# One second-layer tile of the last group but one, moved within the last group's V products

## The chip, the cores and the metric

The kernel runs on one core of one Trainium2 chip. The metric is the device time of one execution in microseconds (us). A core has five engines that run on their own and wait for each other through counters: TensorE (PE; its weight loads are shown as PEld), VectorE (DVE), ScalarE (ACT), GpSimd (POOL) and SyncE (SP), which here only issues copies. Each engine works through its own queue in order.

## The reference

The input x has 16 x 512 rows of 512 numbers. Each row carries a pathway number (0 to 499), a compartment number (0 to 4) and a mask bit; each batch entry has three condition vectors.

```
h = ln(x, pw_g[pathway], pw_b[pathway]);  h = ln(h, cp_g[compartment], cp_b[compartment])
t = ln(x, tm_g[compartment], tm_b[compartment])
m, n, r = x + mlp_ln(condition)            # one vector per batch entry and condition
s = ln(x, ms_g[mask], ms_b[mask])
cat = concat(w0*h, w1*t, w2*m, w3*n, w4*r, w5*s)        # w = softmax(aw)
out = x + ln(silu(cat @ W1 + b1) @ W2 + b2) * g + be    # W1: 3072 x 512, W2: 512 x 512
```

All is in float32. The kernel does not form the concatenation. What depends on x alone goes through one 512 x 512 matrix (the X product: the weighted sum of three blocks of W1); t and s are the same normalized x times table rows, so for rows of one (compartment, mask) pair they go through one blended matrix (the V product); h goes through its own block (the H product). What is left, constant for a pair and a batch entry, is one row that is added.

## The kernel before

The 8192 rows are sorted by (mask, compartment) pair and cut into 16 groups of 512 rows (`sts`, one state per group); a group is worked on as four tiles of 128 rows (`NJ` = `Q` = 4). A preparation, ordered by a list of pieces written out by hand, sorts the rows, computes tables and conditions, and does the first two groups. A loop of 16 steps per group does the next ones (`step`), and `last_window` does the last group, number 15, together with what is left of group 14. The schedule is manual: instructions stand in each engine's queue in the order in which the program emits them, and the framework adds the waits.

The first layer of a group is twelve products, X, V and H for each of its four tiles: `layer1` (L300, matmul in L305), four matrix instructions of a 128 x 128 block against 128 x 512 each, which show as eight records in the profile. They accumulate in one PSUM tile per row tile; the result is complete after the H product. The left operands (`cX`, `cV`, `cH`) are transposed rows; VectorE transposes 32 x 32 blocks into `rX`, `rV`, `rH`, and SP copies them into place, 16 copies of 64 KB per operand (`spread`, L164).

The V product of tile g needs the blended matrix for that tile, in four parts: ScalarE writes one scaled table block (`s_part`, L190), VectorE multiplies and adds the other (`build`, L196). Two buffers `vs` serve for this; in the last group the third matrix lies in a buffer of x that is free by then (it appears as `xbs`).

The hidden tile takes its gathered row (`hidden_add`, L309), SiLU (L312), a transposition and a spread into `cZ`; the second layer (`layer2`, L322, matmul in L324) makes four matrix instructions per tile, against W2, into another PSUM pool of four buffers. After it come an addition (L327), the sum of squares on ScalarE (L332), the inverse root on GpSimd (L345, a power), scale and residual on VectorE, and an indirect output from GpSimd (`put_out`, L358). GpSimd also adds the output offset to x in place, once per tile (`shift_x`, L294), and issues the gathers (L130).

In `last_window` the steps s = 0 to 11 emit the products X0 to X3, V0 to V3, H0 to H3 of group 15. `end_hidden` at step 0 finishes group 14's hidden tiles and spreads its `cZ`. The builds for V1 and V2 are emitted in step 3, that for V3 in step 6; the shifts of the four tiles in steps 4 to 7, each after the gather of steps 3 to 6. The nested function `finish` does everything from the second layer to the output for one tile. For tile 0 of group 14 it is called at step 8, before H0 is emitted; for the other three, and for the four of group 15, behind the loop.

Of the kernel before, what the change touches and what calls it, by code (L numbers as in the profile page):

```python
# [52 lines left out]
def kernel(ctx: ExitStack, tc: tile.TileContext, a: dict, out: bass.AP):  # L53
# [26 lines left out]
    NJ = S // P  # L80
# [78 lines left out]
    def spread_row(st, rot, cat, blk, g):  # L159

        if cat not in st:
            st[cat] = catp.tile([P, Q, NC, P], F32, tag=f"cat{blk}", name=f"{cat}{st['w']}")
        for q in range(Q):
            nc.sync.dma_start(st[cat][q * L : (q + 1) * L, g].rearrange("p c t -> p (c t)"),  # L164
                              st[rot][g * L : (g + 1) * L, q].rearrange("p c j t -> p (c j t)"))

    def spread(st, blk):
        for g in range(Q):
            spread_row(st, "r" + blk, "c" + blk, blk, g)
# [15 lines left out]
    def s_part(st, g, at=None):  # L185

        w = st["w"]
        st["v", g] = v = vs[(Q * w + g) % 2] if at is None else at
        for c in range(NC):
            nc.scalar.activation(v[:, c], ws[:, c], AF.Identity, scale=scs[:, c, g, w : w + 1])  # L190

    def build(st, g):
        w = st["w"]
        v = st["v", g]
        for c in range(NC):
            nc.vector.scalar_tensor_tensor(v[:, c], wt[:, c], sct[:, c, g, w : w + 1], v[:, c], ALU.mult, ALU.add)  # L196

    def gather_add(st, g):
        w = st["w"]
        st["add", g] = t = gp.tile([P, D], F32, tag="add", name=f"add{w}_{g}", bufs=4)  # L200
        gather(t, rows_2[:, :], i_add[:, g, w : w + 1])
# [76 lines left out]
    def front_a(st, j):  # L278
        norm_n(st, j)
        front_1(st, j)  # L280
        front_pow(st, j)

    def front_b1(st, j):
        front_mean(st, j)
        front_norm(st, j)

    def front_b2(st, j):
        pw, cp = st.pop(("g", j))
        nc.vector.tensor_mul(pw[:, :D], pw[:, :D], cp)  # L289
        turn_to(st, "rH", "H", j, pw[:, :D])  # L290

    def shift_x(st, j):

        nc.gpsimd.tensor_add(st["xb"][:, j, :], st["xb"][:, j, :], rows[:, 2, :])  # L294


    def psum(k, name):
        return (ps_1, ps_2)[k].tile([P, D], F32, tag=("p1", "p2")[k], name=name)

    def layer1(st, blk, g):  # L300
        if blk == "X":
            st["p1", g] = psum(0 if st["w"] == 0 else 1, f"p1_{st['w']}_{g}")
        m = {"X": wx_, "V": st.get(("v", g)), "H": wh_}[blk]
        for c in range(NC):
            nc.tensor.matmul(st["p1", g], st["c" + blk][:, g, c, :], m[:, c, :],  # L305
                             start=(blk == "X" and c == 0), stop=(blk == "H" and c == NC - 1))
# [7 lines left out]
    def hidden(st, g):  # L314
        hidden_add(st, g)
        hidden_silu(st, g)

    def turn_z(st, g, blk="Z"):
        turn_to(st, "rZ", blk, g, st["add", g])

    def layer2(st, j):
        st["p2", j] = p2 = psum(0, f"p2_{st['w']}_{j}")  # L322
        for c in range(NC):
            nc.tensor.matmul(p2, st["cZ"][:, j, c, :], w2[:, c, :], start=(c == 0), stop=(c == NC - 1))  # L324
# [9 lines left out]
    def last_a(st, j):  # L334
        last_add(st, j)
        last_sum(st, j)
# [10 lines left out]
    def last_std(st, lo=0, hi=NJ):  # L347
        last_var(st, lo, hi)
        last_pow(st, lo, hi)
# [6 lines left out]
    def put_out(st, j):  # L356
        w = st["w"]
        nc.gpsimd.indirect_dma_start(out_rows, bass.IndirectOffsetOnAxis(ap=tok[:, j, w : w + 1], axis=0),  # L358
                                     yb[:, j, :], None)
# [52 lines left out]
    for nm in ("mem", "noi", "res"):  # L412
        k = a[nm + "T"].shape[0]
# [479 lines left out]
    def end_hidden(st, older):  # L893

        last_b(older, 3)
        hidden(st, 3)
        turn_z(st, 2)
        turn_z(st, 3)
        spread(st, "Z")
# [86 lines left out]
    def last_window(older, prev, st):  # L986

        def finish(done, j):

            y = yb[:, j, :]  # L990
            layer2(done, j)
            last_a(done, j)
            yg = gp.tile([P, D], F32, tag="cp", name=f"yg{done['w']}_{j}")
            nc.vector.tensor_mul(yg, y, rows[:, 1, :])
            last_std(done, j, j + 1)
            nc.vector.scalar_tensor_tensor(y, yg, done["rsy"][:, j : j + 1], done["xb"][:, j, :], ALU.mult, ALU.add)
            put_out(done, j)

        for s in range(13):
            if s == 8:  # L1000
                finish(prev, 0)
            if s < 12:
                layer1(st, "XVH"[s // 4], s % 4)
            if s == 0:
                end_hidden(prev, older)
            elif s == 1:
                put_out(older, 2)
                front_a(st, 2)
                s_part(st, 2, older["xb"])
            elif s == 2:  # L1010
                put_out(older, 3)
                front_b1(st, 2)
                front_a(st, 3)
                front_b2(st, 2)
            elif s == 3:
                front_b1(st, 3)
                build(st, 1)
                front_b2(st, 3)
                spread(st, "H")
                build(st, 2)  # L1020
            elif s == 5:
                s_part(st, 3, vs[Q * st["w"] % 2])
            elif s == 6:
                build(st, 3)
            elif s >= 9:
                hidden(st, s - 9)
                if s >= 10:
                    turn_z(st, s - 10, "V")
            if 3 <= s < 7:
                gather_add(st, s - 3)  # L1030
            if 4 <= s < 8:
                shift_x(st, s - 4)
        turn_z(st, 3, "V")
        for g in range(Q):
            spread_row(st, "rZ", "cZ", "V", g)
        for j in range(1, NJ):
            finish(prev, j)
        for j in range(NJ):
            finish(st, j)

    for w in range(2, NW - 1):
        for s in range(16):
            step(s, *sts[w - 2 : w + 3])
    last_window(*sts[NW - 3 : NW])


# [51 lines left out]
```

## Time and profile before

| | us |
|---|---|
| median of 3 runs | 1045.17 (1044.87 to 1051.08) |
| profiled execution | 1045.43 |
| its span, first to last instruction | 1043.4 |
| TensorE busy in the span | 994.1 (95%) |
| VectorE, ScalarE, GpSimd busy | 877.9, 572.7, 572.2 |
| mean granted TensorE clock | 0.982 of full |
| last group's X products begin | 960.05 |
| last product ends | about 1033 |

A row of the order-of-time view has the start in us from the span's start, the length in us, the engine, the line, the operation, "written tile <- read tiles" with the size, and the number of instructions merged; in brackets stands the engine's idle time just before and what ended it. Ends of matrix instructions are modelled, so starts are the firmer numbers. SP's copies are shown as SPq. Busy time on GpSimd is rough.

### The profile page before, as it was taken

The page shows a single profiled execution, that of the slowest core. Times are in us where ns is not written, and L with a number is a line of the kernel's source. Part 1 is how long each engine was busy: PE and PEld are TensorE (multiplying, and loading weights), DVE is VectorE, ACT ScalarE, POOL GpSimd, SP SyncE. Part 2 cuts the span into 40 slices and gives each one's busy share as a digit, 9 for nine tenths or more (in the row PEclk, how much of TensorE's full clock was granted, in tenths as well). Part 3 has the DMA queues.
Part 4 walks back from the last instruction along what each step waited for, and adds up shares of the span by engine and source line. Part 5 has one row for each costly group of instructions (what it writes and reads, how often), then busy time and mean ns, then how long its engine had stood idle before and what let it go on. Part 6 is the DMA issues. An engine that isn't in the chain of part 4 may idle for free.

```text
span 1043.4 us, 11015 instructions
## 1 busy us (share of the span) xinstructions
PE 994.1 (95%) x2523; PEld 450.3 (43%) x2523; DVE 877.9 (84%) x1577; ACT 572.7 (55%) x1153; POOL 572.2 (55%) x573
## 2 busy tenths in 40 slices
PE   5989699899999999999999999999999999999896
PEld 5634244343344444444444444444444444444342
DVE  7978889888889888888888888888888989888844
ACT  2698684483746473646464555546374647364311
POOL 3764652645656574737464646555565656473413
PEclk9979999899999999999999999999999999999998
DMA  9595887666767585767666676667677768585512
GB/s 276 196 269 159 236 260 218 166 182 184 197 182 215 160 232 157 226 166 205 174 199 181 193 188 192 183 203 190 194 195 193 200 171 227 154 229 152 146 35 91
DMA packets 95655, 197.66 MB, mean 189 GB/s; under 512 B 26290, under 2 KB 26290, under 8 KB 95592
## 3 DMA queue, kind: packets, MB, share of 16 engines
q0 software_dynamic: 32096, 108.55, 36.4%
q1 hardware_dynamic: 62230, 87.44, 30.3%
q10 hardware_dynamic: 1266, 0.99, 0.3%
q8 instruction: 21, 0.34, 0.1%
q14 instruction: 42, 0.34, 0.1%
HBM read 104.14 MB, written 21.44 MB: 120 GB/s over the span
## 4 chain that ended last, share of the span: by engine, by line
PE 70%; DVE 11%; DMA 4%; ACT 4%; issue 4%; SPq 3%; POOL 2%; POOLq 0%; DVEq 0%; ACTq 0%
PE p L305 48%; PE p L324 16%; SPq L164 3%; PE pe L811 3%; DVE vs L196 3%; PE pn L574 2%; DVE pw L289 1%; DMA xbs<-in_mem_W 1%; ACT vs L190 1%; ACT pw L276 1%; DVE add L309 1%; DVE yb L353 1%; DMA add<-rows,i_add 1%; POOL xbs L130 1%; DVE pw L260 1%
## 5 line engine op out<-in xcount | busy, mean ns | idle before, releaser
L305 PE MATMUL p<-vs,cV 128*128 128x512 f32 x504 | 229.6, 600 | 5.6 <-DVE vs L196 5.6
L324 PE MATMUL p<-w,cZ 128*128 128x512 f32 x512 | 228.9, 592 | 0.0
L305 PE MATMUL p<-wx__82,cX 128*128 128x512 f32 x512 | 225.8, 599 | 2.0 <-DVE add L309 2.0
L305 PE MATMUL p<-wh__83,cH 128*128 128x512 f32 x512 | 222.8, 592 | 0.0
L196 DVE SCALAR_TENSOR_TENSOR vs<-wt,sct,vs 128x512 f32<-128x512 f32 x252 | 206.3, 877 | 0.0
L190 ACT ACTIVATE vs<-ws,scs 128x512 f32<-128x512 f32 x252 | 160.7, 707 | 2.6 <-PE pe L811 2.1
L269 POOL TENSOR_TENSOR rsh<-veh,mhalf 128x1 f32<-128x1 f32 x64 | 46.0, 719 | 198.0 <-DVE veh L265 190.1
L305 PEld LDWEIGHTS p<-wx__82,cX 128*128 128x128 f32 x512 | 98.2, 192 | 125.7 <-issue 119.0
L305 PEld LDWEIGHTS p<-vs,cV 128*128 128x128 f32 x504 | 95.7, 192 | 130.5 <-issue 95.1
L324 PEld LDWEIGHTS p<-w,cZ 128*128 128x128 f32 x512 | 97.3, 190 | 122.6 <-issue 121.3
L305 PEld LDWEIGHTS p<-wh__83,cH 128*128 128x128 f32 x512 | 97.3, 190 | 122.5 <-issue 121.7
L276 ACT ACTIVATE pw<-pw,nmh,rsh 128x512 f32<-128x512 f32 x64 | 51.8, 809 | 128.4 <-DVE nmh L147 128.4
L312 ACT ACTIVATE add<-add 128x512 f32<-128x512 f32 x64 | 40.3, 630 | 145.4 <-DVE add L309 141.1
L358 POOL DMA_INDIRECT out<-yb,tok x64 | 68.5, 1070 | 64.4 <-DVE yb L353 27.5
L332 ACT ACTIVATE junk<-yb 128x512 f32<-128x512 f32 x64 | 40.1, 627 | 95.1 <-DVE yb L327 94.9
L130 POOL DMA_INDIRECT add<-rows,i_add x64 | 75.9, 1185 | 24.1 <-issue 9.1
L260 DVE TENSOR_TENSOR pw<-xn,pw 128x512 f32<-128x512 f32 x64 | 44.0, 688 | 48.5 <-ACT xn L237 48.5
L294 POOL TENSOR_TENSOR xbs<-xbs,rows 128x512 f32<-128x512 f32 x64 | 81.4, 1275 | 0.9
L130 POOL DMA_INDIRECT xbs<-in_x,tok x64 | 65.1, 1017 | 24.6 <-issue 18.0
L130 POOL DMA_INDIRECT cp<-cp_rows,i_cp x64 | 67.8, 1060 | 19.5 <-issue 19.2
L130 POOL DMA_INDIRECT pw<-in_pw,i_pw x64 | 64.0, 1000 | 20.9 <-issue 12.7
L237 ACT ACTIVATE xm<-xbs,mnm,mrs 128x512 f32<-128x512 f32 x64 | 48.6, 804 | 41.3 <-DVE rV L156 39.0
(234 smaller groups left out, 1236.8 us busy)
## 6 DMA issues: line engine op xcount, KB each, us to landing
cX<-rX SPq DMA_DIRECT2D x256, 64.0 KB
cV<-rV SPq DMA_DIRECT2D x256, 64.0 KB
cH<-rH SPq DMA_DIRECT2D x256, 64.0 KB
cZ<-rZ SPq DMA_DIRECT2D x256, 64.0 KB
cVe<-rVe SPq DMA_DIRECT2D x64, 64.0 KB
rows<-adde SPq DMA_DIRECT2D x14, 256.0 KB
w1x<-in_int_W SPq DMA_DIRECT2D x2, 1024.0 KB
ws<-in_int_W SPq DMA_DIRECT2D x1, 1024.0 KB
```

The costliest lines, as they stand in the source:

```text
L130: nc.gpsimd.indirect_dma_start(dst, None, table, bass.IndirectOffsetOnAxis(ap=idx, axis=0), **kw)
L190: nc.scalar.activation(v[:, c], ws[:, c], AF.Identity, scale=scs[:, c, g, w : w + 1])
L196: nc.vector.scalar_tensor_tensor(v[:, c], wt[:, c], sct[:, c, g, w : w + 1], v[:, c], ALU.mult, ALU.add)
L237: nc.scalar.activation(t, st["xb"][:, j, :], AF.Identity, bias=st[nm][:, j : j + 1], scale=st[rs][:, j : j + 1])
L260: nc.vector.tensor_mul(pw[:, :D], st.pop(("xn", j)), pw[:, :D])
L269: nc.gpsimd.tensor_tensor(rs, st.pop(("ve", j)), mhalf[:, :1], ALU.pow)
L276: nc.scalar.activation(pw[:, :D], pw[:, :D], AF.Identity, bias=st.pop(("nm", j)), scale=st.pop(("rs", j)))
L294: nc.gpsimd.tensor_add(st["xb"][:, j, :], st["xb"][:, j, :], rows[:, 2, :])
L305: nc.tensor.matmul(st["p1", g], st["c" + blk][:, g, c, :], m[:, c, :], start=(blk == "X" and c == 0), stop=(blk == "H" and c == NC - 1))
L312: nc.scalar.activation(st["add", g], st["add", g], AF.Silu)
L324: nc.tensor.matmul(p2, st["cZ"][:, j, c, :], w2[:, c, :], start=(c == 0), stop=(c == NC - 1))
L358: nc.gpsimd.indirect_dma_start(out_rows, bass.IndirectOffsetOnAxis(ap=tok[:, j, w : w + 1], axis=0), yb[:, j, :], None)
```

## The change

The call of `layer2` leaves `finish` and becomes a call of its own. For tile 0 of group 14 it is made at step 6, before V2 is emitted; the rest of `finish` for that tile is called at step 7, after V3 is emitted, where step 8 called all of it before H0. In the queues this gives:

- TensorE: the second-layer tile stands between V1 and V2; before, it stood between V3 and H0.
- VectorE and ScalarE: the same order as before.
- GpSimd: the power (L345) and the output (L358) of that tile stand ahead of the shift of group 15's fourth tile; before, they stood behind it.
- SP: the same order as before.

For the other seven tiles `layer2` is called directly before `finish`, in one loop in place of two, so their order is the same. The functions called are not altered.

```
         def finish(done, j):
             y = yb[:, j, :]
-            layer2(done, j)
             last_a(done, j)
...
         for s in range(13):
-            if s == 8:
-                finish(prev, 0)
+            if s == 6:
+                layer2(prev, 0)
             if s < 12:
                 layer1(st, "XVH"[s // 4], s % 4)
...
             elif s == 6:
                 build(st, 3)
+            elif s == 7:
+                finish(prev, 0)
             elif s >= 9:
...
-        for j in range(1, NJ):
-            finish(prev, j)
-        for j in range(NJ):
-            finish(st, j)
+        for k in range(1, 2 * NJ):
+            done, j = (prev, st)[k // NJ], k % NJ
+            layer2(done, j)
+            finish(done, j)
```

## The prediction

> **What bounds the kernel now.** The page first: which engine fills the span, and what the chain that ended last runs through.
>
> ```profile
> span 1043.4 us, 11015 instructions
> PE 994.1 (95%) x2523; PEld 450.3 (43%) x2523; DVE 877.9 (84%) x1577; ACT 572.7 (55%) x1153; POOL 572.2 (55%) x573
> ```
>
> TensorE is busy for 95% of the span, and the chain gives PE 70%. A change that keeps the number of products can win only where TensorE stands still, so the next view is the order of time on PE over the last group.
>
> ```profile
> 973.78 7.17 PE L305 MATMUL p<-vs,cV 128*128 128x512 f32 x16
> 982.52 1.98 PE L305 MATMUL p<-xbs,cV 128*128 128x512 f32 x4 [1.57 <-DVE xbs L196]
> 986.43 1.98 PE L305 MATMUL p<-xbs,cV 128*128 128x512 f32 x4 [1.93 <-DVE xbs L196]
> 988.25 3.60 PE L305 MATMUL p<-vs,cV 128*128 128x512 f32 x8
> 991.69 3.60 PE L324 MATMUL p<-w,cZ 128*128 128x512 f32 x8
> 995.12 13.90 PE L305 MATMUL p<-wh__83,cH 128*128 128x512 f32 x32
> 1008.85 24.20 PE L324 MATMUL p<-w,cZ 128*128 128x512 f32 x56
> ```
>
> The rows are V products 0 and 1, the first half of V2, its second half, V3, the second-layer tile in question, the four H products, and the seven remaining second-layer tiles. V2 waits twice for the build of its weights (L196 into xbs); everything else follows back to back. A tile takes 3.43 us (991.69 to 995.12; the H row gives 13.73 / 4). The idle times in brackets are counted against modelled ends, so I count starts: the last record of V1 starts at 980.36 and records follow each other every 0.43 us, so the next could start at 980.79. From there to the H products at 995.12 there are 14.33 us and three tiles of work (V2, V3, one second-layer tile), 10.30 us. TensorE loses 4.03 us here.
>
> Why does V2 wait? VectorE and GpSimd in the same stretch:
>
> ```profile
> 981.04 5.99 DVE L196 SCALAR_TENSOR_TENSOR xbs<-wt,sct,xbs 128x512 f32<-128x512 f32 x4
> 986.96 2.73 DVE L196 SCALAR_TENSOR_TENSOR vs<-wt,sct,vs 128x512 f32<-128x512 f32 x4
> 995.32 0.69 DVE L327 TENSOR_TENSOR yb<-p,rows 128x512 f32<-128x512 f32 x1 [5.63 <-PE p L324]
> ```
> ```profile
> 980.64 1.27 POOL L294 TENSOR_TENSOR xbs<-xbs,rows 128x512 f32<-128x512 f32 x1
> 982.07 1.25 POOL L130 DMA_INDIRECT add<-rows,i_add  x1 [0.16 <-issue]
> 983.33 2.49 POOL L294 TENSOR_TENSOR xbs<-xbs,rows 128x512 f32<-128x512 f32 x2
> 997.10 0.56 POOL L345 TENSOR_TENSOR rsy<-vey,mhalf 128x1 f32<-128x1 f32 x1 [11.28 <-DVE vey L340]
> ```
>
> The same four instructions take 2.73 us for V3's weights and 5.99 us for V2's. One by one: part 0 of V2 981.04 to 982.46 (1.42), part 1 982.39 to 983.13 (0.74), part 2 983.05 to 986.38 (3.33), part 3 986.30 to 987.04 (0.74). Both long ones end 0.55 to 0.56 us after a GpSimd addition of L294 does (981.91 and 985.82): VectorE waits for GpSimd's addition, and beside the indirect load (982.07) it does not. Part 2 waits out two additions, the third and the fourth shift of x, back to back.
>
> **The change, part by part.** *The second-layer tile goes ahead of V2.* The work on TensorE is the same, 3.43 us, at another place. Its weight load needs row 0 of cZ, whose four copies left SP from 966.77 on, 16 in 10.07 us, so by 969.3. SP issues without a gap although each copy waits for the eighth before it, so a copy lands within 8 x 0.63 = 5.0 us (an estimate from the rows of SP): 974.3, 6.5 us ahead of 980.79. Its PSUM buffer was last read by group 13's first second-layer addition, 937.00. So it runs from 980.79 to 984.22.
>
> *V2 behind it.* Part 0 of its weights is ready at 982.46, part 1 at 983.13: no wait at 984.22. Part 2 is wanted half a tile later, at 985.94. When is it ready? This depends on GpSimd, whose queue the change also alters.
>
> *finish moves from ahead of H0 to step 7.* Its VectorE instructions keep their place in that queue (behind the build of V3's weights, ahead of the first hidden addition), and ScalarE's too. On GpSimd the power of L345 and the output of L358 now stand ahead of the fourth shift. The power waits for VectorE, so the fourth shift no longer follows the third at 984.6. Part 2 is then blocked by one addition: 983.33 + 1.27 + 0.55 = 985.15. Part 3 follows at 985.8, V3's parts from 986.5 to 988.45.
>
> Here a rule bears on the sum. The Trainium skill (SBUF — State Buffer, Who interferes with whom) says that a VectorE instruction with two SBUF inputs and a GpSimd instruction that reads SBUF exclude each other, and that the one to issue first keeps the port for its whole length. The exclusion agrees with the rows; the order doesn't: part 2 is recorded at 983.05, the shift at 983.33, and it is part 2 that takes 3.33 instead of 0.74. By the rule part 2 would be ready at 983.8, by the row at 985.15. Both are before 985.94. If the block lasted as long as it does now (something other than the fourth shift), part 2 would be ready at 986.38, 0.4 late, plus about 0.2 for restarting (the first record after a wait is 0.1 longer): that is the upper bound, and V3 would start at 988.25 as now. I take the row.
>
> *The sum.* V2 984.22 to 987.65, V3 to 991.08 (its parts are wanted at 987.65, 988.5, 989.4, 990.2 and ready before), and H0 starts at 991.08 instead of 995.12: 4.04 us. With the block as now it starts at 991.69: 3.43 us.
>
> *What H wants.* Row 0 of cH leaves SP from 981.18, four copies by 983.7, landed by 988.7 by the same 5.0; the later rows need 2.5 us each and are consumed in 3.43. No wait.
>
> *finish's own chain.* From L327 to the end of its output it takes 995.32 to 999.77, 4.45 us, now beginning with the end of the V3 build, 988.45, to 992.9. VectorE is free at 991.6; the first hidden addition is wanted at 991.08 + 3.43 = 994.51, so 2.9 us of cover; without it each us late would move that addition, and VectorE stands idle for over 2 us before each of the next three. The fourth shift follows at 992.9 to 994.2 and is first wanted by the last tile's finish, over 30 us later. ACT, waiting for the same chain, has nothing queued that is wanted before H0 ends. Zero, and a gain isn't possible either, since no one on the path waits for these.
>
> *Rewritten loop.* The seven remaining tiles keep their order: zero.
>
> *What is late next.* From H0 on everything hangs on TensorE: four H products, hidden additions, the spread of cZ, seven tiles, and the outputs. The outputs start at 1015.92, 1019.97, 1024.02, 1027.65, 1031.23, 1034.85 and 1038.45, each only when the one before has landed (the second waits 1.70 for the transfer of the first), so the end is set by that series, not by the last product; but the series begins with tile 1 behind the H products, so it moves with them. I see nothing in it that is tied to an absolute time. The page's span 1043.4 becomes 1039.4; the profiled execution took 1045.43, 2.03 outside the span, and becomes 1041.4; it lies 0.26 above the median of the runs, 1045.17, which becomes 1045.17 - 4.04 = 1041.1.
>
> **The rivals.**
>
> *The block lasts as now*, 3.43 us of gain: 1041.7. For it: VectorE's record starts ahead of GpSimd's, so the account of which instruction holds what is not clean, and spans on GpSimd are rough. Against it: ends at 0.55 us after GpSimd's in both cases, and 0.61 in the build of V1's weights (977.66 to 979.82, addition to 979.21).
>
> *H0 becomes the wait.* Before, H0 is shown not to wait at 995.12, and nothing in the trace shows cH's landing. If it landed only around 993 to 995, between 2 us and nothing would remain: 1043 to 1045.2. Against it: SP's steady issue bounds the landing.
>
> *Slower.* TensorE runs in order, so a late operand of the moved tile holds V2, V3 and all H. The copies of cZ and cH count on the same completion counters; if the wait of the moved tile took in row 0 of cH as well, issued by 983.7, it would start at 986.6 with the 2.9 us that the outputs take to land, at 988.7 with 5.0; H0 10.30 us later, 996.9 to 999.0: 1.8 to 3.9 us slower, I take 1.8, 1047.0. It turns to slower when the tile starts later than 984.8. Against it: in earlier groups the same tile stands one product earlier (922.28, behind V0) and does not wait, with 16 copies of cZ issued from 911.82: 10.5 us after the first, here 14.
>
> *The change doesn't do what it says.* The built order shows it on TensorE, and the GpSimd swap, as described; only the gaps themselves could be a peculiarity of this execution, and then nothing is won: 1045.2. Since they follow from fixed orders of three queues, I put this with the second.
>
> **How the numbers follow.** Full gain 0.64 (1041.1); block as now 0.20 (1041.7); H0 waits or no gap 0.10 (1043 to 1045.2); slower 0.04 (1047.0); something else 0.02. The range reaches from 1040.3 (the full gain and the 0.12 that V1's last part waits, with 0.6 for the scatter of runs, of which the two lower ones lie 0.3 apart) to 1042.8 (the second case with the same scatter, and part of the third). All cases lie within 1%, 10.5 us, about what a measurement of this kernel can tell from no change: faster by more 0.01, within 0.97, slower by more 0.02.
>
> **What would show it.** In the changed kernel's profile: no idle time before the V2 products, the tile of L324 between V1 and V2, starting near 980.8; four xbs builds in about 4.8 instead of 5.99 us, none of 3.33; the fourth shift alone at about 993; H products near 991.1 without idle time; outputs 4 us earlier at equal distances. Wrong it would be if the moved tile waits, if xbs still shows a 3 us part, if idle time appears ahead of H0, or if the outputs' distances grow in exchange.

## The result, and the profile after

| | before | after |
|---|---|---|
| median of 20 runs each, us | 1045.24 (1042.10 to 1051.35) | 1039.88 (1035.46 to 1045.04) |
| ratio, 95% interval | | 0.9952 (0.9937 to 0.9967) |
| profiled execution, us | 1045.43 | 1036.91 |
| its span | 1043.4 | 1034.9 |
| TensorE busy in the span | 994.1 | 987.2 |
| mean granted TensorE clock | 0.982 | 0.988 |

The ratio puts the gain at 5.0 us, between 3.4 and 6.6. The prediction was a gain of 4.04 us, which lies in this interval; of its time, 1041.1 with a range from 1040.3 to 1042.8, the measured median lies 1.2 us below 1041.1 and 0.4 us below the lower end. So there are two questions: did the change do what was worked out, and where does the rest come from? The profiles answer the first and bear on the second, if the span is cut into pieces.

The order of time on PE over the last group, after the change (start, length, engine, line, operation, number merged):

```profile
955.73 13.90 PE L305 MATMUL p<-wx__82,cX 128*128 128x512 f32 x32
969.46 7.03 PE L305 MATMUL p<-vs,cV 128*128 128x512 f32 x16
976.33 3.60 PE L324 MATMUL p<-w,cZ 128*128 128x512 f32 x8
979.76 3.60 PE L305 MATMUL p<-xbs,cV 128*128 128x512 f32 x8
983.20 3.60 PE L305 MATMUL p<-vs,cV 128*128 128x512 f32 x8
986.63 13.90 PE L305 MATMUL p<-wh__83,cH 128*128 128x512 f32 x32
1000.36 24.20 PE L324 MATMUL p<-w,cZ 128*128 128x512 f32 x56
```

No row has a bracket: the view shows no wait of TensorE here any more. The second-layer tile stands between V1 and V2, and V2 is one row instead of two halves. From the X products to the H products it takes 986.63 - 955.73 = 30.90 us; before, it took 995.12 - 960.05 = 35.07. The difference is 4.17 us.

VectorE and GpSimd beside it, after the change:

```profile
976.56 4.79 DVE L196 SCALAR_TENSOR_TENSOR xbs<-wt,sct,xbs 128x512 f32<-128x512 f32 x4
981.27 2.73 DVE L196 SCALAR_TENSOR_TENSOR vs<-wt,sct,vs 128x512 f32<-128x512 f32 x4
983.92 0.68 DVE L327 TENSOR_TENSOR yb<-p,rows 128x512 f32<-128x512 f32 x1
```
```profile
978.85 1.28 POOL L294 TENSOR_TENSOR xbs<-xbs,rows 128x512 f32<-128x512 f32 x1
985.69 0.56 POOL L345 TENSOR_TENSOR rsy<-vey,mhalf 128x1 f32<-128x1 f32 x1 [5.56 <-DVE vey L340]
987.32 1.03 POOL L358 DMA_INDIRECT out<-yb,tok  x1 [1.08 <-DVE yb L995]
988.38 1.28 POOL L294 TENSOR_TENSOR xbs<-xbs,rows 128x512 f32<-128x512 f32 x1
```

The build of V2's weights has shrunk from 5.99 to 4.79 us, since the fourth shift now runs alone at 988.38, behind the power and the output. The addition L327 no longer waits 5.63 us for TensorE.

From the H products to the end of the span it takes 1034.9 - 986.63 = 48.27 us, before 1043.4 - 995.12 = 48.28. The last group therefore explains 4.18 us of a difference of 8.5 us between the two spans. The other 4.32 us are ahead of it. The X products of the groups, before and after (rows of the order of time on PE):

```profile
300.85 13.90 PE L305 MATMUL p<-wx__82,cX 128*128 128x512 f32 x32
960.05 13.90 PE L305 MATMUL p<-wx__82,cX 128*128 128x512 f32 x32
```
```profile
296.53 13.90 PE L305 MATMUL p<-wx__82,cX 128*128 128x512 f32 x32
955.73 13.90 PE L305 MATMUL p<-wx__82,cX 128*128 128x512 f32 x32
```

The first row of each pair is group 3, the second group 15. Between them lie 659.20 us in both kernels. The 4.3 us are already there at group 3, in the preparation and the first groups, whose program the change doesn't touch. This is scatter of an execution, unless something makes it lasting; the experiments were to tell.

### The profile page after: what moved, and what is told of

Read it like the earlier page. It is cut to its first block, busy times and chain, and to the rows that moved or that the text cites. A ratio compares the mean times of both kernels' runs of the same rounds, so it can differ in the third digit from the quotient of the medians.

```text
span 1034.9 us, 11013 instructions
## 1 busy us (share of the span) xinstructions
PE 987.2 (95%) x2523; PEld 447.5 (43%) x2523; DVE 876.2 (85%) x1577; ACT 572.7 (55%) x1153; POOL 570.4 (55%) x573
## 4 chain that ended last, share of the span: by engine, by line
PE 82%; DVE 5%; DMA 4%; ACT 3%; issue 3%; SPq 1%; POOL 1%; POOLq 0%; DVEq 0%; ACTq 0%
PE p L305 57%; PE p L324 19%; PE pe L811 3%; PE pn L574 1%; SPq L164 1%; DMA xbs<-in_mem_W 1%; DMA out<-yb,tok 1%; PE ph L549 1%; DMA adde<-rows,i_addx 1%; DMA cH<-rH 1%; DVE vs L196 1%; DMA xbs<-in_x,tok_x 1%; DVE pw L289 0%; ACT vs L190 0%; DVE vs L805 0%
## 5 line engine op out<-in xcount | busy, mean ns | idle before, releaser
L196 DVE SCALAR_TENSOR_TENSOR vs<-wt,sct,vs 128x512 f32<-128x512 f32 x252 | 206.3, 878 | 0.0
L358 POOL DMA_INDIRECT out<-yb,tok x64 | 68.2, 1066 | 63.8 <-DVE yb L353 26.9
L130 POOL DMA_INDIRECT add<-rows,i_add x64 | 75.6, 1182 | 22.8 <-issue 9.7
L130 POOL DMA_INDIRECT xbs<-in_x,tok x64 | 65.4, 1022 | 24.8 <-issue 17.8
L130 POOL DMA_INDIRECT cp<-cp_rows,i_cp x64 | 68.0, 1062 | 19.5 <-issue 19.2
L130 POOL DMA_INDIRECT pw<-in_pw,i_pw x64 | 64.0, 1000 | 22.2 <-issue 12.7
```

What stands on the lines that cost most here:

```text
L130: nc.gpsimd.indirect_dma_start(dst, None, table, bass.IndirectOffsetOnAxis(ap=idx, axis=0), **kw)
```

## The experiments

Two theories and their rivals: first, that GpSimd's additions block the build of V2's weights, that the moved tile covers most of the wait and the swap on GpSimd the rest (rivals: VectorE's own load sets the build, or the tile alone does everything). Second, that the gain is about 4.2 us and all beyond it is scatter of the front part (rival: the front is lastingly shorter).

The expectations are given for the time from group 3's X products to the end of the span. In the runs the middle part, groups 3 to 14, turned out to scatter too, so the table cuts the span in three: front (to the start of group 3's X products), middle (to the start of group 15's), last (to the end of the span). For the unaltered kernel before, the expectation's 742.55 is 659.20 + 83.35; 738.4 in an expectation answers to 79.2 in the last column. Each row of the table is one profiled execution. Where two profiles of one kernel exist, their last parts differ by 0.1 (after) and 0.4 us (before), so differences in the last column are good to a few tenths.

| run | span | front | middle | last |
|---|---|---|---|---|
| before | 1043.4 | 300.85 | 659.20 | 83.35 |
| before, again | 1045.7 | 303.55 | 659.20 | 82.95 |
| after | 1034.9 | 296.53 | 659.20 | 79.17 |
| after, again | 1040.4 | 301.79 | 659.33 | 79.28 |
| tile alone | 1044.4 | 303.30 | 661.23 | 79.87 |
| fourth shift alone | 1039.4 | 297.12 | 660.24 | 82.04 |
| all shifts behind, tile not moved | 1040.3 | 299.60 | 661.52 | 79.18 |
| all shifts behind, tile moved | 1037.3 | 298.53 | 659.56 | 79.21 |
| tile ahead of X3 | 1037.1 | 296.31 | 660.32 | 80.47 |
| two tiles moved | 1037.7 | 299.28 | 659.44 | 78.98 |
| two outputs left out | 1039.0 | 302.65 | 659.20 | 77.15 |

### The tile alone

```
             if s == 6:
                 layer2(prev, 0)
+            if s == 8:
+                finish(prev, 0)
             if s < 12:
                 layer1(st, "XVH"[s // 4], s % 4)
...
             elif s == 6:
                 build(st, 3)
-            elif s == 7:
-                finish(prev, 0)
             elif s >= 9:
```

> The second-layer tile stands between V1 and V2 as in the changed kernel, but finish is called at step 8 again, so on GpSimd the fourth shift follows the third at once, as in the kernel before. Measure: time from the start of group 3's X products to the end of the span, 742.55 us before and 738.37 after; the part ahead of it scatters between executions. Theory (GpSimd's additions block the build of V2's weights, the tile covers most of it, the delayed fourth shift the rest): the third xbs build takes 3.3 us again, V2 waits 0.4 to 0.6 at its middle, 738.9 to 739.1. Rival (the swap on GpSimd is without effect, the tile does it all): 738.4 and no wait in V2.

The last part takes 79.87 us, 3.48 less than in the first profile of the kernel before (3.08 less than in its second) and 0.6 to 0.7 more than after the change. The order of time on PE and VectorE in this run:

```profile
988.65 1.88 PE L305 MATMUL p<-xbs,cV 128*128 128x512 f32 x4
990.87 1.98 PE L305 MATMUL p<-xbs,cV 128*128 128x512 f32 x4 [0.34 <-DVE xbs L196]
```
```profile
987.48 3.33 DVE L196 SCALAR_TENSOR_TENSOR xbs<-wt,sct,xbs 128x512 f32<-128x512 f32 x1
```

The third part of the build takes 3.33 us again, and V2 waits at its middle: by starts, 990.87 - (988.65 + 1.72) = 0.50 us. This is the case that the prediction had given as its first rival, 3.43 us. The whole time from group 3 on, 741.1, was off the expectation of 738.9 to 739.1 because the middle part took 2.03 us longer than in the kernel before: two of its groups took 55.62 and 56.20 us instead of 54.93, without any change there. In both groups, as in the long groups of the other runs, TensorE stops ahead of a V product for a build of L196 (at 503.02 for 0.42 us, at 718.98 and 724.10 for 0.17 and 0.56); the seven executions without a long group show no such stop in the middle part. In the first of the two the build is no longer than usual (4.16 us), but begins 25.59 us after the group's X products instead of 24.87 one group earlier. What made VectorE late there was not followed.

### The fourth shift alone

```
             if s == 8:
                 finish(prev, 0)
+                shift_x(st, 3)
...
-            if 4 <= s < 8:
+            if 4 <= s < 7:
                 shift_x(st, s - 4)
```

> The kernel before, with nothing altered but the fourth shift, which is emitted behind finish of step 8; the second-layer tile stays ahead of H0. Same measure. Theory: the third xbs build waits for one addition instead of two, about 2.1 instead of 3.33 us, V2's second wait shrinks by 1.2, the first stays: 741.3. Rival (VectorE's own load sets the build): xbs builds as before, 742.5.

```profile
979.77 1.98 PE L305 MATMUL p<-xbs,cV 128*128 128x512 f32 x4 [1.57 <-DVE xbs L196]
982.47 1.98 PE L305 MATMUL p<-xbs,cV 128*128 128x512 f32 x4 [0.72 <-DVE xbs L196]
```
```profile
980.30 2.12 DVE L196 SCALAR_TENSOR_TENSOR xbs<-wt,sct,xbs 128x512 f32<-128x512 f32 x1
```

The first wait is as before, the second 0.72 instead of 1.93, and the third part takes 2.12 instead of 3.33: 1.21 us less in both. The last part is 82.04 us, 1.31 less than in the first profile of the kernel before (0.91 less than in its second), as the theory expects. (From group 3 on it is 742.28, because the middle took 1.04 longer.) Against the two profiles of the kernel before, the tile alone is worth 3.1 to 3.5 us and the swap alone 0.9 to 1.3; the whole change, against the same two, is worth 3.7 to 4.2. The two halves do not add up: the tile covers most of the wait, and beside it the swap brings only the 0.6 to 0.7 us that the cover leaves.

### All four shifts behind, the tile not moved

```
             if s == 8:
                 finish(prev, 0)
+                for j in range(NJ):
+                    shift_x(st, j)
...
-            if 4 <= s < 8:
-                shift_x(st, s - 4)
```

> The kernel before with all four shifts emitted behind finish of step 8, so that no addition of GpSimd runs beside the builds; the second-layer tile stays ahead of H0. Same measure. Theory: all builds at 0.66 us a part (2.7 for four), V2's weights are ready when V1 ends, no wait, 738.4, the same as the change without moving the tile. Rival (VectorE's own load): at least one wait of V2 stays, 740 to 742.5.

```profile
976.67 2.73 DVE L196 SCALAR_TENSOR_TENSOR vs<-wt,sct,vs 128x512 f32<-128x512 f32 x4
980.67 2.70 DVE L196 SCALAR_TENSOR_TENSOR xbs<-wt,sct,xbs 128x512 f32<-128x512 f32 x4
983.29 2.73 DVE L196 SCALAR_TENSOR_TENSOR vs<-wt,sct,vs 128x512 f32<-128x512 f32 x4
```
```profile
974.86 7.03 PE L305 MATMUL p<-vs,cV 128*128 128x512 f32 x16
981.73 3.60 PE L305 MATMUL p<-xbs,cV 128*128 128x512 f32 x8
985.16 3.60 PE L305 MATMUL p<-vs,cV 128*128 128x512 f32 x8
988.59 3.60 PE L324 MATMUL p<-w,cZ 128*128 128x512 f32 x8
```

With no addition of GpSimd beside them, all three builds take 2.7 us, 0.75 at most per part, and TensorE doesn't wait although the tile still stands ahead of H0. The last part takes 79.18 us: the same as with the change. (From group 3 on it is 740.70 instead of the 738.4 expected, because the middle took 2.32 longer.) The ratio of this kernel to the one before is 0.9947 (0.9924 to 0.9971) in 10 runs. This shows GpSimd's additions to be the cause of the wait: the third part of the build takes 0.75, 2.12 and 3.33 us beside none, one and two of them, and the rival of VectorE's own load, by which a wait of V2 had to stay, falls.

One thing the prediction did not read: the first wait of V2 has its origin one build earlier, too. In the kernel before, the build of V1's weights is stretched by the first shift:

```profile
975.67 4.10 DVE L196 SCALAR_TENSOR_TENSOR vs<-wt,sct,vs 128x512 f32<-128x512 f32 x4
```

It takes 4.10 us there and 2.73 here, so V2's build begins 20.99 us after the X products there and 19.55 here. With the shifts away, both this delay and the 0.68 us of V2's own first part (1.42 instead of 0.74) are gone.

### All four shifts behind, the tile moved

```
             elif s == 7:
                 finish(prev, 0)
+                for j in range(NJ):
+                    shift_x(st, j)
...
-            if 4 <= s < 8:
-                shift_x(st, s - 4)
```

> The changed kernel with all four shifts emitted behind finish of step 7: both covers at once. Same measure. Theory: TensorE has no idle time left in the last group after the change, so nothing more is won: 738.3 to 738.4. Rival (something is still lost beside the builds): below 738.

The last part takes 79.21 us, the same within 0.1. Either of the two, the moved tile with the swap or all four shifts behind, is enough, and with one of them nothing is left to win at this place.

### Both kernels again

> The changed kernel again, unaltered, to see whether the front part of the execution, which the change doesn't touch, differs from the kernel before in a lasting way. Measure: start of group 3's X products (300.85 us before, 296.53 after in the profiled executions) and time from there to the end of the span (742.55 and 738.37). Theory (the gain is 4.2 us, and what the medians show beyond it is scatter of the front part): 738.3 to 738.5 behind, the front anywhere from 295 to 305. Rival (the change also shortens the front by about 1 us or more): the front again near 296.5, and the ratio again near 0.995.

> The kernel before again, unaltered, under the same measure as a changed one: what no change looks like. Theory: 742.5 us behind, the front 295 to 305; the ratio within 0.2% of 1. Rival (the front part of the kernel before is lastingly longer): the front 300 or more.

The last part repeats: 79.28 and 82.95 us (before, the first wait of V2 was 1.37 instead of 1.57, and V1's last part didn't wait, which makes 0.34 of the 0.40). The front does not: the unaltered changed kernel now reaches group 3 at 301.79, 5.3 us later than in its first profile and later than the first profile of the kernel before. Over the eleven profiles, all with the same program up to there, the front lies between 296.31 and 303.55. The repeated kernels measured 0.9955 (0.9932 to 0.9979) for the change and 1.001 (0.9988 to 1.0031) for no change, 12 runs each. The rival of a lastingly shorter front had named two signs: the front near 296.5 again, which did not come, and a ratio near 0.995 again, which did. A single front of 301.79 shows that 4.3 us are not lasting; among fronts that lie 7 us apart it can't exclude one of those that are shorter by 1 us. The mean front is 300.3 us in the four profiles with the tile ahead of H0 and 299.8 in the seven others: no difference that such a spread would let one see.

Why the front scatters was not tried. The granted TensorE clock varies there, but its first stretch does not sort the executions. The first 57 us of the first profile before, the first after and the second after, with fronts of 300.85, 296.53 and 301.79 (a table by stretches: bounds, length, PE busy and instructions, granted clock, DMA share, GB/s):

```profile
0.00:57.00 57.00, 42.37 (x295) 0.94 0.74 235
```
```profile
0.00:57.00 57.00, 42.46 (x311) 0.97 0.74 238
```
```profile
0.00:57.00 57.00, 40.90 (x311) 1.00 0.73 238
```

The execution with the full clock here has the longest front of the three. Between 100 and 150 us the granted clock is 0.97 in the four profiles with the shortest fronts, and 0.90, 0.90, 0.90 and 0.93 in the four with the longest; nothing here shows whether it is cause or effect.

### The tile ahead of X3

```
-            if s == 6:
+            if s == 3:
                 layer2(prev, 0)
```

> The changed kernel with the second-layer tile emitted ahead of X3, three products earlier. TensorE gets there about 1.1 us after SP has issued the last of the four copies of cZ row 0, so the wait that it shows measures when these copies have landed, which the prediction only bounded (5.0 us at most). With 2 to 3 us to land: a wait of 1 to 2 us ahead of X3; with 5.0: 3.9 us. The time from group 3's X products to the end grows by as much over 738.4, since the cover for V2 stays: 739.4 to 742.3.

```profile
968.22 3.67 PE L324 MATMUL p<-w,cZ 128*128 128x512 f32 x8 [1.12 <-DMA cZ<-rZ]
```

TensorE waits 1.12 us ahead of the moved tile, and the last part grows by 1.2 to 1.3. SP had begun to issue cZ at 963.36, and the chain that ended last shows the fourth copy's transfer:

```profile
965.18 2.90 DMA cZ<-rZ
968.09 0.14 issue
```

Row 0 is complete 4.73 us after SP began, 2.9 after its last copy was issued. The prediction had bounded this by 5.0 us for each copy; in the changed kernel the tile begins 14.0 us after SP does (976.33 against 962.29). So a late operand of the tile does hold everything behind it, as the slower rival of the prediction said, once the tile stands too early; at the place chosen there are 9 us to spare.

### Two tiles moved

```
-            if s == 6:
-                layer2(prev, 0)
+            if s in (6, 8):
+                layer2(prev, (s - 6) // 2)
...
+            elif s == 8:
+                finish(prev, 1)
...
-        for k in range(1, 2 * NJ):
+        for k in range(2, 2 * NJ):
```

> The changed kernel with the second tile of group 14 moved too: its second layer stands between V3 and H0, its finish behind; so six outputs instead of seven are left behind the H products, and two tiles of second layer instead of three cover the spread of the last group's cZ. Theory (the end is set by outputs that wait for one another, each 3.6 us against 3.43 of a tile on TensorE): the last output follows its tile without waiting for the one before, 1 to 1.9 us less, against a wait of TensorE ahead of group 15's first second-layer tile of 0 to 1.0: 736.5 to 738.0. Rival (the end is set by TensorE's last product alone): 738.4 or, with the wait, up to 739.4.

The last part takes 78.98 us (738.42 from group 3 on), 0.2 to 0.3 less than with the change, and TensorE doesn't wait. The time is near the rival's, but its reason doesn't fit the rows: the first output behind the H products starts at 1013.89, the next at 1017.93, 1021.58, 1025.59, 1029.22 and 1032.83. They still wait for one another, 18.94 us for five steps where five tiles take 17.2 on TensorE. One output fewer saves one step's excess over a tile, not the wait as such: here the expectation was wrong. In the times this kernel can't be told from the changed one (0.9966, 0.9940 to 0.9992, in 12 runs).

### Two outputs left out

```
-            put_out(done, j)
+            if (done["w"], j) not in ((NW - 2, 3), (NW - 1, 1)):
+                put_out(done, j)
```

> The changed kernel with the outputs of tile 3 of group 14 and of tile 1 of group 15 left out (this part of the computation is missing from the result, everything ahead of it is computed). Measure: from the start of group 15's X products to the end of the span, 79.2 us in the changed kernel. Theory (behind the last product the end hangs on outputs that each wait for the one before, 3.6 us and more against 3.43 of a tile): with two fewer, the last output follows its tile at once or up to 0.3 later, 1.5 to 1.9 us less, 77.3 to 77.7. Rival (the last tile's own chain from TensorE to the output sets the end, as the small gain of the moved second tile suggests): 79.0 to 79.2.

The last part takes 77.15 us, 2.0 to 2.1 less: a little more than the 1.5 to 1.9 expected, and far from the rival's 79.0. The power and the output of the last tile in the changed kernel, and then here:

```profile
1027.48 0.57 POOL L345 TENSOR_TENSOR rsy<-vey,mhalf 128x1 f32<-128x1 f32 x1
1029.97 1.03 POOL L358 DMA_INDIRECT out<-yb,tok  x1 [1.93 <-issue]
```
```profile
1032.51 0.56 POOL L345 TENSOR_TENSOR rsy<-vey,mhalf 128x1 f32<-128x1 f32 x1 [0.81 <-DVE vey L340]
1034.21 1.03 POOL L358 DMA_INDIRECT out<-yb,tok  x1 [1.15 <-DVE yb L995]
```

Counted from the seven tiles' first start (1000.36 and 1006.49), the last output starts at 29.61 and at 27.72. In the changed kernel the power waits behind the output ahead of it in GpSimd's queue (at 1026.36, not shown, busy for 1.09); here it waits for VectorE alone. So the series of outputs does set the end, as the prediction said, and is worth 2 us behind the last product.

## Why the prediction was right, and where it was wrong

**The waits of V2 as the only loss.** Right for the last group. 4.03 us were counted between V1's last record and H0. From the X products to H0 the change won 4.17 us by the first two profiles, 4.04 with the second profile after, 3.83 with the second before and 3.70 with both second ones: 3.9 on average. Part of the spread is the wait of V1's last part, which the prediction named in its range and which comes and goes: V0 and V1 together show 7.17 and 7.03 us before, 7.03 and 7.16 after.

**Each start.** Counted from group 15's X products, predicted (from 960.05) and measured (from 955.73): the moved tile 20.74 and 20.60, V2 24.17 and 24.03, V3 27.60 and 27.47, H0 31.03 and 30.90. All differ by the same 0.13 or 0.14, the wait of V1's last part. In the second profile after, which has that wait, they are 20.73, 24.16, 27.60 and 31.03: the predicted numbers within 0.01.

**GpSimd's part.** Right: four xbs builds in 4.79 us (4.8 predicted), the fourth shift at 32.65 us from the X products (32.85 predicted), finish's chain to the end of its output at 32.62 (32.85). Part 2 of the build after the change:

```profile
978.57 2.12 DVE L196 SCALAR_TENSOR_TENSOR xbs<-wt,sct,xbs 128x512 f32<-128x512 f32 x1
```

It is ready at 978.57 + 2.12 - 955.73 = 24.96 us from the X products; 25.10 was predicted. The row was the better guide than the rule: the Trainium skill (SBUF — State Buffer, Who interferes with whom) has the exclusion right, 0.75, 2.12 and 3.33 us beside none, one and two additions, but by its order, first to issue keeps the port, part 2 would have run through in 0.74, since its record starts 0.28 us ahead of the addition's (978.57 and 978.85 after, 983.05 and 983.33 before). It is the addition that runs through, in 1.28 us. Whether a record's start on VectorE is the moment at which it asks for the port stays open.

**The first rival, block as now.** It gave 3.43; the tile alone, which has that block, won 3.1 to 3.5. Its chance of 0.20 was spent on a doubt that the earlier rows, each ending 0.55 to 0.57 us after an addition, did not support. (The third of them was given as 0.61 with an end at 979.82; by its row, 977.66 and 2.12 long, it ends at 979.78, 0.57 after the addition.)

**H0 as the wait, and the slower case.** Neither came: no idle time ahead of H0, none ahead of the moved tile. The moved tile starts at 976.33, 0.37 us before SP begins to issue cH (976.70), so its wait does not take in the copies of cH, on which the slower case rested. The bound of 5.0 us for SP's copies held; 2.9 were measured for the last of four.

**The end.** Right: the outputs keep their distances (1007.42 to 1029.97, 22.55 us, against 22.53), and the part from H0 to the end differs by 0.01 us.

**The step that failed is the term for the scatter in the range.** The prediction took "0.6 for the scatter of runs, of which the two lower ones lie 0.3 apart", passing over the third of its three runs, 5.9 us away; the lower end was 1041.1 less 0.12 less 0.6 (1040.4 by these terms, stated as 1040.3). Over 20 runs the standard deviation is 2.5 us for the kernel before and 2.7 after, so that the median of 20 is itself uncertain by some 0.7 us, and a difference of two such medians by about 1. The measured 5.36 us between the medians is about 4 us of the last group (3.7 to 4.2 by the profiles), and 1.2 to 1.7 us for which nothing lasting was found. That is why the measured median fell out of the range at its lower end, while the predicted ratio, 0.9961, lies between 0.9937 and 0.9967. With the scatter of the 20 runs, about 1.5 us to either side of the same sum would have been needed, 1039.6 to 1042.6, for the median after alone. The sum also stood on the median of three runs, 1045.17; that the median of 20 lies only 0.07 from it was luck.

Whether scatter is all of it stays open: the prediction expected no change ahead of the last group, and the runs don't settle this. That the rest is scatter is argued from the front's spread of 7.2 us in eleven profiles. Against it stands that the rest came back: the changed kernel twice, all shifts behind with the tile not moved, and two tiles moved, each with a last part of about 79 us, have ratios of 0.9952, 0.9955, 0.9947 and 0.9966 in 10 to 20 runs. These are 5.0, 4.7, 5.6 and 3.6 us, three of them above 4.2. Each of the four intervals includes 4.2 us. The times alone leave a further effect of up to 2.4 us open.

## What to carry to other kernels

Where one engine is the bound and waits for one late operand, work that is ready and has no order to keep can stand in the gap; here it cost nothing, since its own operands had landed 9 us before. Taking away what makes the operand late, the additions beside the build, was worth the same. Look at the same instruction's time in different places first: four builds in 2.7 us here and 6.0 there, beside the rows of the other engines, name the culprit, an addition on GpSimd, where the chain of waits shows only the late build. And when the predicted gain is smaller than the distance between runs, cut the span at a row that the change can't move, and compare the parts: here the last part repeats within 0.4 us where the times of one kernel differ by 9. A range for a median then has to come from that distance, and not from the two runs that happen to agree.

## What the runs showed of the hardware that was not expected

- A VectorE build part of 128x512 in float32, 0.74 us by itself, takes 2.12 us beside one addition of GpSimd of 1.27 and 3.33 beside two back to back: it gets no turn between them. The addition keeps its 1.27 to 1.28 us, although the record of the build part starts 0.28 us earlier. An indirect load on GpSimd (L130, 1.25 us) beside it costs nothing: the part then takes 0.74 us.
- Indirect outputs that must keep their order follow each other at 3.6 to 4.1 us, though each keeps GpSimd for only 1.0 to 1.5. Behind the last product this was worth 2.0 us.
- Unaltered code takes 296.3 to 303.6 us for the first 29% of the execution. The twelve later periods of 54.93 us repeat within 0.02 us in four of the eleven executions; in four others one or two of them are 0.7 to 1.3 us longer.
